# A state-space recurrence in two halves a step, with its outputs half a step late

## Chip, cores and metric

One core of one Trainium2 chip runs the whole program. The metric is device time in microseconds; before the change it was 1826.9 us, the median of three runs (1825.44 to 1828.99).

## What is computed

The layer is a Mamba block followed by a mixture of experts, each with a residual and a layer norm, on 4 sequences of 1024 tokens of width 256, all in float32. Shortened, and with the two norms left as names:

```python
h = rmsnorm(x) @ w_in                          # 256 -> 1024
xs, res = split(h)                             # 512 channels each
res = silu(res)                                # the gate
xs = silu(causal_conv4(xs))
delta, B, C = split(xs @ w_xproj)              # 16, 16 and 16 columns
delta = softplus(delta @ w_dt + b_dt)
# for each channel and each of the 16 states n, along time t:
#   s[t] = exp(delta[t] * A[n]) * s[t-1] + delta[t] * xs[t] * B[n, t]
y = sum over n of s[n] * C[n]
x1 = layernorm(2 * x + ((y + xs * D) * res) @ w_out)
# experts: one shared, and the best 2 of 8 for each token, weighted
out = layernorm(x1 + shared(norm(x1)) + routed(norm(x1)))
```

## The kernel before

The tokens are worked in eight chunks of 512, two to a sequence. Channels lie on partitions: 512 channels are four tiles of 128, so a value for all channels of a chunk is a 128x2048 tile. The loop at the end of the kernel goes over 128 steps, (sequence, chunk, state n). The engines are TensorE (PE), VectorE (DVE), ScalarE (ACT), GpSimd (POOL) and SyncE (SP). A step has four parts, each a small function:

- `over_partitions` (L383): PE copies one row of B or C onto all partitions, in a PSUM tile `pb`.
- `inputs` (L391): ACT copies the B row (`b`, L395); DVE multiplies three of the four channel tiles with it (L397), POOL the fourth (L401). The result is `hs`, of which three buffers exist.
- `scan` (L404): for each channel tile, ACT makes the decay `da` = exp(delta * A) (L409) in one of two PSUM buffers, and DVE runs the scan over time in `hs` (L412). In a sequence's first chunk, ACT then keeps the last column in `state` (L421) for the second.
- `outputs` (L417): DVE multiplies `hs` with the C row in place (L422), and POOL adds the product to `y` (L423).

Around the steps, generators are advanced a piece at a time by `other_work`, which the loop calls twice a step:

- `front` prepares the next chunk: its norm, the projection, the convolution (taps at L302), SiLU of xs (L323), the projections and softplus. Its inner generator `gate` (L280) is started in the chunk's own loop at n = 1; it projects the gate, copies it (L286) and applies SiLU (L288) into `res`, of which there is one buffer.
- `tail` ends a chunk: y times res (L435, on POOL), the output projection (`po`, L446), the layer norm with its square root (`rsqrt`, L194 to L207, twelve small POOL operations after two on DVE), and the router. `by_expert` then sorts the tokens to experts: DVE works out rows and counts in the PSUM tile `pr`; POOL scatters the rows to DRAM by four indirect DMAs for each of a token's two choices (`scatter`, L580 to L592) and makes `there` and `ee` (L609, L611), from which DVE makes a plan of blocks (L615 and after).
- `moe` works off the expert blocks on PE with weights loaded from DRAM by SP: `up` (L748, L755) and `down` (L769, L797), and adds the results to DRAM by POOL's DMAs (L788, L800). Blocks of a chunk are worked during the following chunk's steps; those of the last chunk come after the last step.

The kernel is written in the order of the program; a scheduler then decides each engine's order by what is ready, and pools decide which buffer comes free when. Each engine takes its instructions in order. An ACT function of another table set than the last makes the compiler put a table load ahead of it.

Of the kernel before, what the change touches and what calls it, by code (L numbers as in the profile page):

```python
# [9 lines left out]
AF = mybir.ActivationFunctionType  # L10
# [6 lines left out]
N = 16  # L17
# [5 lines left out]
TC = 512  # L23
NCH = SEQ // TC
TT = TC // P
KD = D // P
KB = DI // P
# [30 lines left out]
def mamba_moe_kernel(  # L58
# [18 lines left out]
    nc = tc.nc  # L77
# [13 lines left out]
    def load_x(b, c):  # L91
        t = two.tile([P, TT, D], F32, tag="x", name=f"x_{b}_{c}", bufs=3)
        nc.sync.dma_start(t, x[b, c * TC : (c + 1) * TC, :].rearrange("(t p) d -> p t d", p=P))
        return t
# [71 lines left out]
    state = const.tile([P, KB, N], F32, tag="state", name="state")  # L166
# [16 lines left out]
    def fill(g):  # L183

        nc.sync.dma_start(sums_of[g][0:P, :], empty[:, 0:D])
        rows = rows_of[g].rearrange("(n p) d -> p n d", p=P)
        for n in range(0, NS // P, 14):
            some = min(14, NS // P - n)
            nc.sync.dma_start(
                rows[:, n : n + some, :], empty.unsqueeze(1).to_broadcast([P, some, W])  # L190
            )
            yield
# [49 lines left out]
    xs_in, gates, scans, channels, routes = {(0, 0): first_x}, {}, {}, {}, {}  # L242
    chunks = [(b, c) for b in range(NSEQ) for c in range(NCH)]
# [4 lines left out]
    def front(b, c):  # L248
# [22 lines left out]
        def projected(m):  # L271
            pi = ps_mix.tile([P, TC], F32, tag="mix", name=f"pi_{s}_{m}")
            for k in range(KD):
                nc.tensor.matmul(  # L274
                    pi, lhsT=w_in_sb[:, k, m * P : (m + 1) * P], rhs=hT[:, k, :],
                    start=(k == 0), stop=(k == KD - 1),
                )
            return pi

        def gate():  # L280

            res = one.tile([P, KB, TC], F32, tag="res", name=f"res_{s}")
            for m in range(KB):
                pi = projected(KB + m)
                yield
                nc.scalar.copy(res[:, m, :], pi)  # L286
                yield
            nc.scalar.activation(res, res, AF.Silu)  # L288
            gates[b, c] = res


        xs = two.tile([P, KB, TC], F32, tag="xs", name=f"xs_{s}")
# [15 lines left out]
        if c > 0:  # L308
            come = one.tile([P, KB, K - 1], F32, tag="come", name=f"come_{s}")
            part = one.tile([P, KB, K - 1], F32, tag="come1", name=f"come1_{s}")  # L310
            for back in range(K - 1, 0, -1):
                to = come if back == K - 1 else part
                nc.gpsimd.tensor_tensor(
                    to[:, :, 0:back], halo[:, :, K - 1 - back :],
                    chan_sb[:, :, CW + K - 1 - back : CW + K - back].to_broadcast([P, KB, back]),
                    ALU.mult,
                )
                if back < K - 1:
                    nc.gpsimd.tensor_tensor(
                        come[:, :, 0:back], come[:, :, 0:back], part[:, :, 0:back], ALU.add  # L320
                    )
            nc.gpsimd.tensor_tensor(xs[:, :, 0 : K - 1], xs[:, :, 0 : K - 1], come, ALU.add)
        nc.scalar.activation(xs, xs, AF.Silu)  # L323


# [53 lines left out]
    def over_partitions(step, row):  # L379

        b, c, n = step
        pb = ps_mix.tile([P, TC], F32, tag="mix", name=f"pb_{b}_{c}_{row}")
        nc.tensor.matmul(  # L383
            pb, lhsT=pick[:, row : row + 1].to_broadcast([P, P]), rhs=scans[b, c][3],
            start=True, stop=True,
        )
        return pb
# [3 lines left out]
    def inputs(step, pb):  # L391
        b, c, n = step
        xs = scans[b, c][0]
        copy = two.tile([P, TC], F32, tag="b", name=f"b_{b}_{c}_{n}")
        nc.scalar.copy(copy, pb)  # L395
        hs = wide.tile([P, KB, TC], F32, tag="s", name=f"hs_{b}_{c}_{n}")
        nc.vector.tensor_tensor(  # L397
            hs[:, 0:on_pool, :], xs[:, 0:on_pool, :],
            pb.unsqueeze(1).to_broadcast([P, on_pool, TC]), ALU.mult,
        )  # L400
        nc.gpsimd.tensor_tensor(hs[:, on_pool, :], xs[:, on_pool, :], copy, ALU.mult)  # L401
        return hs

    def scan(step, hs):  # L404
        b, c, n = step
        delta = scans[b, c][1]
        for k in range(KB):
            da = ps_da.tile([P, TC], F32, tag="da", name=f"da_{b}_{c}_{n}_{k}")
            nc.scalar.activation(  # L409
                da, delta[:, k, :], AF.Exp, scale=chan_sb[:, k, CA + n : CA + n + 1]  # L410
            )
            nc.vector.tensor_tensor_scan(  # L412
                hs[:, k, :], da, hs[:, k, :], 0.0 if c == 0 else state[:, k, n : n + 1],
                ALU.mult, ALU.add,
            )

    def outputs(step, hs, pb):  # L417
        b, c, n = step
        y = scans[b, c][2]
        if c + 1 < NCH:  # L420
            nc.scalar.copy(state[:, :, n : n + 1], hs[:, :, TC - 1 : TC])  # L421
        nc.vector.tensor_tensor(hs, hs, pb.unsqueeze(1).to_broadcast([P, KB, TC]), ALU.mult)  # L422
        nc.gpsimd.tensor_tensor(y, y, hs, ALU.add)  # L423

# [129 lines left out]
    def by_expert(b, c, hn, rank, weights, both, part, flat):  # L554
# [6 lines left out]
        place = part(TT + 1, E)  # L561
# [18 lines left out]
        def scatter(i):  # L580
            nc.gpsimd.tensor_copy(hn[:, :, WEIGHT : WEIGHT + 1], weights[:, i, :].unsqueeze(2))
            for t in range(TT):
                ins = nc.gpsimd.indirect_dma_start(
                    rows_of[g][:, :],
                    bass.IndirectOffsetOnAxis(to[:, i, t : t + 1].bitcast(U32), 0),
                    hn[:, t, :], None,
                ).ins
                for other in scatters:
                    tc.declare_no_dep(ins, other, reason="no two choices share a row")
                for other in taken_from[g]:  # L590
                    tc.declare_no_dep(ins, other, reason="rows behind those of full blocks")
                scatters.append(ins)  # L592

        scatter(0)

        if not at:
            done_of[g] = one.tile([P, E], F32, tag="done", name=f"done_{g}")
# [11 lines left out]
        nc.gpsimd.tensor_tensor(there, there, done, ALU.subtract)  # L609
        ee = one.tile([P, E, E], F32, tag="ee", name=f"ee_{s}")  # L610
        nc.gpsimd.tensor_tensor(ee, before, there.unsqueeze(1).to_broadcast([P, E, E]), ALU.mult)  # L611
        yield
        scatter(1)
        base, ends, first, whose, first_of = part(E), part(E), part(E), part(blocks), part(blocks)
# [5 lines left out]
        of = flat[:, 0 : blocks * E].rearrange("p (a b) -> p a b", a=blocks)  # L620
        step = steps[:, 0:blocks]
# [242 lines left out]
    order = [(b, c, n) for b, c in chunks for n in range(N)]  # L864
    done, beside, work = [], [], moe()
    at_once = 2.0

    def advance(count):
        for _ in range(count):
            if not next(work, False):  # L870
                return False
        return True

    def side():
        for g in list(beside):
            if next(g, "end") == "end":
                beside.remove(g)
        while done:
            beside.append(finish(done.pop(0)))
# [3 lines left out]
    def other_work():  # L883
        nonlocal owed
        side()
        owed += at_once
        while owed >= 1.0:
            owed = owed - 1.0 if advance(1) else 0.0

    for _ in front(0, 0):  # L890
        pass
    xs_in[0, 1] = load_x(0, 1)
    hs = inputs(order[0], over_partitions(order[0], 0))
    for i, step in enumerate(order):
        b, c, n = step
        over_c = over_partitions(step, N + n)
        if i + 1 < len(order) and n + 1 < N:
            over_b = over_partitions(order[i + 1], n + 1)
        scan(step, hs)
        place = chunks.index((b, c))  # L900
        if n == 1:
            beside.append(scans[b, c][4]())
        if n == 2 and place < NGROUP:
            beside.append(fill(place))
        if n == 2 and place + 1 < len(chunks):
            beside.append(front(*chunks[place + 1]))
        other_work()
        if i + 1 < len(order):
            if n + 1 == N:
                over_b = over_partitions(order[i + 1], 0)  # L910
            ahead = inputs(order[i + 1], over_b)
        outputs(step, hs, over_c)
        hs = ahead
        if n == N - 1:
            beside.append(tail(b, c))
            if place + 2 < len(chunks):
                xs_in[chunks[place + 2]] = load_x(*chunks[place + 2])
        other_work()
    working = True
    while working or beside or done:  # L920
        working = next(work, None) is not None
# [56 lines left out]
```

## Time and profile before

| | us |
|---|---|
| median of three runs | 1826.9 |
| profiled execution | 1829.25 |
| its span (first to last instruction) | 1827.6 |
| first scan | 72.5 |
| end of the recurrence, about | 1530 |

The profile is of one execution and gives, per engine, the busy time, groups of instructions by source line, and the waits with the instruction that ended each. The costliest groups, each with its count, busy time and mean of one: L423 (POOL, y) x128, 589.7 us, 4607 ns; L409 (ACT, da) x512, 350.5 us, 696 ns; L412 (DVE, scan) x512, 616.6 us, 1270 ns with a kept state and 1209 ns without; L422 (DVE, C product) x128, 291.9 us, 2280 ns; L397 (DVE, B product) x128, 222.3 us, 1737 ns; L401 (POOL) x128, 176.9 us, 1383 ns. A mean granted PE clock of 0.83 is listed for the core. Idle time counts where it is on the engine that sets the pace of its stretch; elsewhere it costs nothing.

### The profile page before, as it was taken

How to read it: one execution, taken by the hardware profiler on the slowest of the kernel's cores; microseconds unless marked ns; L12 is line 12 of the kernel's file. 1: busy time of each engine (PE TensorE's matmuls, PEld its weight loads, DVE VectorE, ACT ScalarE, POOL GpSimd, SP SyncE). 2: the span in 40 equal slices, each digit the busy share in tenths (PEclk: the TensorE clock that was granted, in tenths of full speed). 3: DMA queues.
4: the chain of work that ended last, by engine and by line, in shares of the span. 5: the costliest groups of instructions: out<-in, count | busy, mean ns of one | idle time of the engine just before them, and what ended most of it. 6: DMA issues, size and time to landing. Idle time of an engine off the chain costs nothing. (4 is left out here: it accounts for less than half of the span.)

```text
span 1827.6 us, 20355 instructions
## 1 busy us (share of the span) xinstructions
PE 1291.5 (71%) x6366; PEld 974.9 (53%) x6366; DVE 1283.7 (70%) x1369; ACT 1118.2 (61%) x2426; POOL 1160.1 (63%) x901
## 2 busy tenths in 40 slices
PE   4354247734788867886887788777887787999970
PEld 1011025512556645674666466655575677899960
DVE  2599898789878877887798778877988795200003
ACT  5555647564758675866686657856785654444433
POOL 1555774688568965896679756976688675412222
PEclk8555567856798978998998889988998898999995
DMA  9990000300055513652175206720653076399985
GB/s 288 321 317 4 0 12 12 124 6 11 15 154 172 156 38 105 204 160 52 51 231 161 78 24 192 216 74 16 199 169 114 27 224 197 103 319 295 316 238 167
DMA packets 199998, 254.19 MB, mean 139 GB/s; under 512 B 21305, under 2 KB 177090, under 8 KB 199890
## 3 DMA queue, kind: packets, MB, share of 16 engines
q1 hardware_dynamic: 173858, 222.54, 37.9%
q0 software_dynamic: 17648, 21.96, 7.0%
q10 hardware_dynamic: 8384, 8.39, 1.3%
q8 instruction: 50, 0.82, 0.2%
q14 instruction: 58, 0.48, 0.1%
HBM read 185.67 MB, written 67.20 MB: 138 GB/s over the span
## 5 line engine op out<-in xcount | busy, mean ns | idle before, releaser
L423 POOL TENSOR_TENSOR y<-y,hs 128x2048 f32<-128x2048 f32 x128 | 589.7, 4607 | 153.1 <-DVE hs L422 150.9
L409 ACT ACTIVATE da<-delta,chan_sb 128x512 f32<-128x512 f32 x512 | 350.5, 696 | 158.6 <-DVE hs L412 154.8
L769 PE MATMUL pd<-w,h 128*128 128x256 f32 x1648 | 403.6, 389 | 24.6 <-ACT rb L797 11.8
L769 PEld LDWEIGHTS pd<-w,h 128*128 128x128 f32 x1648 | 310.4, 195 | 107.6 <-issue 32.4
L412 DVE TENSOR_TENSOR_SCAN hs<-da,state,hs 128x512 f32<-128x512 f32 x256 | 316.4, 1270 | 59.8 <-ACT da L409 58.5
L412 DVE TENSOR_TENSOR_SCAN hs<-da,hs 128x512 f32<-128x512 f32 x256 | 300.2, 1209 | 62.8 <-ACT da L409 62.4
L748 PEld LDWEIGHTS pu<-xT,w 128*128 128x128 f32 x2272 | 287.0, 205 | 65.2 <-ACT xT L734 46.5
L748 PE MATMUL pu<-xT,w 128*128 128x128 f32 x2272 | 292.5, 290 | 38.2 <-ACT xT L734 34.9
L755 ACT ACTIVATE h<-pu,wb 128x128 f32<-128x128 f32 x824 | 236.0, 374 | 105.2 <-PE pu L748 103.0
L422 DVE TENSOR_TENSOR hs<-hs,pb 128x2048 f32<-128x2048 f32 x128 | 291.9, 2280 | 6.7 <-ACT state L421 3.0
L383 PE MATMUL pb<-parts,pick 128*128 128x512 bf16 x256 | 108.8, 440 | 199.4 <-DVE hs L397 78.2
L397 DVE TENSOR_TENSOR hs<-xs,pb 128x1536 f32<-128x1536 f32 x128 | 222.3, 1737 | 31.6 <-POOL xs L374 23.5
L401 POOL TENSOR_TENSOR hs<-xs,b 128x512 f32<-128x512 f32 x128 | 176.9, 1383 | 99.9 <-ACT b L395 99.2
L800 POOL DMA_INDIRECT sums<-rb,xb x71 | 112.9, 1591 | 178.1 <-issue 86.6
L274 PE MATMUL pi<-hT,w_in_sb 128*128 128x512 f32 x256 | 158.4, 754 | 74.1 <-DVE hs L397 25.6
L748 PEld LDWEIGHTS pu<-x1T,w 128*128 128x128 f32 x1024 | 152.6, 230 | 36.3 <-issue 29.8
L748 PE MATMUL pu<-x1T,w 128*128 128x128 f32 x1024 | 156.4, 315 | 1.6 <-ACT h L755 1.3
L213 DVE BATCH_NORM_STATS2 bnst_l<-o 128x6 f32<-128x256 f32 x32 | 11.9, 412 | 192.0 <-DMA o<-sums 192.0
L274 PEld LDWEIGHTS pi<-hT,w_in_sb 128*128 128x128 f32 x256 | 56.1, 234 | 159.4 <-DVE hs L397 44.8
L395 ACT COPY b<-pb 128x512 f32<-128x512 f32 x128 | 74.9, 585 | 79.2 <-PE pb L383 77.9
L383 PEld LDWEIGHTS <-pick 128*128 128x128 bf16 x256 | 26.6, 107 | 154.1 <-issue 110.5
L446 PE MATMUL po<-w_out_sb,y 128*128 128x256 f32 x256 | 74.3, 454 | 44.8 <-POOL y L435 38.2
(160 smaller groups left out, 1434.8 us busy)
## 6 DMA issues: line engine op xcount, KB each, us to landing
w<-in_ew SPq DMA_DIRECT2D x142, 1024.0 KB, 6.0
rows<-empty SPq DMA_DIRECT2D x19, 1806.0 KB, 18.9
w<-in_sw SPq DMA_DIRECT2D x16, 1024.0 KB, 5.7
xb<-rows SPq DMA_DIRECT2D x71, 129.0 KB, 4.7
x<-in_x SPq DMA_DIRECT2D x8, 512.0 KB, 4.5
sums<-summed ACTq DMA_DIRECT2D x8, 512.0 KB, 2.9
sums<-rs POOLq DMA_DIRECT2D x16, 256.0 KB, 4.8
o<-sums SPq DMA_DIRECT2D x4, 1024.0 KB, 8.0
```

What stands on the lines that cost most here:

```text
L274: nc.tensor.matmul(pi, lhsT=w_in_sb[:, k, m * P : (m + 1) * P], rhs=hT[:, k, :], start=(k == 0), stop=(k == KD - 1),)
L383: nc.tensor.matmul(pb, lhsT=pick[:, row : row + 1].to_broadcast([P, P]), rhs=scans[b, c][3], start=True, stop=True,)
L397: nc.vector.tensor_tensor(hs[:, 0:on_pool, :], xs[:, 0:on_pool, :], pb.unsqueeze(1).to_broadcast([P, on_pool, TC]), ALU.mult,)
L401: nc.gpsimd.tensor_tensor(hs[:, on_pool, :], xs[:, on_pool, :], copy, ALU.mult)
L409: nc.scalar.activation(da, delta[:, k, :], AF.Exp, scale=chan_sb[:, k, CA + n : CA + n + 1])
L412: nc.vector.tensor_tensor_scan(hs[:, k, :], da, hs[:, k, :], 0.0 if c == 0 else state[:, k, n : n + 1], ALU.mult, ALU.add,)
L422: nc.vector.tensor_tensor(hs, hs, pb.unsqueeze(1).to_broadcast([P, KB, TC]), ALU.mult)
L423: nc.gpsimd.tensor_tensor(y, y, hs, ALU.add)
L748: nc.tensor.matmul(pu[:, i, :], lhsT=w[:, k, at : at + P], rhs=xT[:, k, :], start=(k == 0), stop=(k == KD - 1),)
L755: nc.scalar.activation(t[:, i, :], pu[:, i, :], AF.Relu, bias=wb[:, m : m + 1])
L769: nc.tensor.matmul(pd, lhsT=hidden[h][:, i, :], rhs=w[:, m, :], start=(m == 0), stop=(m == HB - 1 and e is None),)
L800: nc.gpsimd.indirect_dma_start(sums_of[g][:, :], bass.IndirectOffsetOnAxis(xb[:, TOKEN : TOKEN + 1].bitcast(U32), 0), rb, None, compute_op ...
```

## The change

A step's scans are split in two: channel tiles 0 and 1, then 2 and 3. Between the halves stand the outputs of the step before, and the first call of other work; the C row is asked for after that call. After the second half the state is kept, the next step's inputs are made, and the second call of other work follows. A chunk's tail and the load of a later x move from the end of the chunk's last step into the first step of the next chunk.

SiLU of the gate leaves `gate` (except for the last chunk) and is written in the following chunk's `front`, directly ahead of SiLU of xs. In `by_expert`, the first `scatter` is written after `there` and `ee`.

```diff
         def gate():
...
-            nc.scalar.activation(res, res, AF.Silu)
             gates[b, c] = res
+            if (b, c) == chunks[-1]:
+                nc.scalar.activation(res, res, AF.Silu)
...
+        place = chunks.index((b, c))
+        if place:
+            gate_before = gates[chunks[place - 1]]
+            nc.scalar.activation(gate_before, gate_before, AF.Silu)
         nc.scalar.activation(xs, xs, AF.Silu)
...
-    def scan(step, hs):
+    def scan(step, hs, of):
...
-        for k in range(KB):
+        for k in of:
...
+    def keep(step, hs):
+        b, c, n = step
+        if c + 1 < NCH:
+            nc.scalar.copy(state[:, :, n : n + 1], hs[:, :, TC - 1 : TC])
+
     def outputs(step, hs, pb):
...
-        if c + 1 < NCH:
-            nc.scalar.copy(state[:, :, n : n + 1], hs[:, :, TC - 1 : TC])
...
-        scatter(0)
...
         nc.gpsimd.tensor_tensor(ee, before, there.unsqueeze(1).to_broadcast([P, E, E]), ALU.mult)
+        scatter(0)
         yield
         scatter(1)
...
+    first, second = range(KB // 2), range(KB // 2, KB)
+    hs, late = inputs(order[0], over_partitions(order[0], 0)), None
     for i, step in enumerate(order):
         b, c, n = step
-        over_c = over_partitions(step, N + n)
-        if i + 1 < len(order) and n + 1 < N:
+        place = chunks.index((b, c))
+        more = i + 1 < len(order)
+        if more and n + 1 < N:
             over_b = over_partitions(order[i + 1], n + 1)
-        scan(step, hs)
-        place = chunks.index((b, c))
+        scan(step, hs, first)
+        if late is not None:
+            outputs(*late)
+            if n == 0:
+                beside.append(tail(*chunks[place - 1]))
+                if place + 1 < len(chunks):
+                    xs_in[chunks[place + 1]] = load_x(*chunks[place + 1])
...
         other_work()
-        if i + 1 < len(order):
-            if n + 1 == N:
-                over_b = over_partitions(order[i + 1], 0)
-            ahead = inputs(order[i + 1], over_b)
-        outputs(step, hs, over_c)
-        hs = ahead
-        if n == N - 1:
-            beside.append(tail(b, c))
-            if place + 2 < len(chunks):
-                xs_in[chunks[place + 2]] = load_x(*chunks[place + 2])
+        over_c = over_partitions(step, N + n)
+        if more and n + 1 == N:
+            over_b = over_partitions(order[i + 1], 0)
+        scan(step, hs, second)
+        keep(step, hs)
+        late = (step, hs, over_c)
+        if more:
+            hs = inputs(order[i + 1], over_b)
         other_work()
+    outputs(*late)
+    beside.append(tail(*chunks[-1]))
```

More of the change, by code (lines that the diff above doesn't have):

```diff
@@ L892, in mamba_moe_kernel @@
     xs_in[0, 1] = load_x(0, 1)
-    hs = inputs(order[0], over_partitions(order[0], 0))
+    first, second = range(KB // 2), range(KB // 2, KB)
+    hs, late = inputs(order[0], over_partitions(order[0], 0)), None
     for i, step in enumerate(order):
         b, c, n = step
-        over_c = over_partitions(step, N + n)
-        if i + 1 < len(order) and n + 1 < N:
+        place = chunks.index((b, c))
+        more = i + 1 < len(order)
+        if more and n + 1 < N:
             over_b = over_partitions(order[i + 1], n + 1)
-        scan(step, hs)
-        place = chunks.index((b, c))
+        scan(step, hs, first)
[5 more added lines that the diff above has]
+                    xs_in[chunks[place + 1]] = load_x(*chunks[place + 1])
         if n == 1:
```

## The prediction

> **What bounds the kernel now.** I read the page's busy shares first, then the busy time by stretch, to see where one engine sets the pace.
>
> ```profile
> span 1827.6 us, 20355 instructions
> ...
> PE 1291.5 (71%) x6366; PEld 974.9 (53%) x6366; DVE 1283.7 (70%) x1369; ACT 1118.2 (61%) x2426; POOL 1160.1 (63%) x901
> ```
>
> No engine looks full over the whole span, but the stretches differ (columns: stretch, its length, then busy PE, PEld, DVE, ACT, POOL, with the PE clock, DMA share and GB/s last):
>
> ```profile
> 72.50:1530.00 1457.50, 1033.62 (x4804) 752.21 (x4803) 1237.47 (x1220) 960.83 (x1991) 1062.29 (x725) 0.82 0.38 112
> 1530.00:1827.00 297.00, 232.16 (x1518) 213.38 (x1518) 29.04 (x119) 116.95 (x360) 73.57 (x121) 0.89 0.76 234
> ```
>
> In the recurrence (72.5 to 1530 us) DVE works 1237.5 of 1457.5 us. One of the 128 steps is four scans, a B product and a C product: 4 x 1.24 + 1.74 + 2.28 = 8.98 us of DVE, 1149 us in all; the rest is the next chunk's convolution and the routing. The last 297 us belong to the expert blocks, PE and weight DMAs, and the change adds or removes nothing there. So the time is DVE's work plus 220 us of DVE idle. Next come DVE's waits in that stretch (total us, times, longest):
>
> ```profile
> DVE hs L412 <- ACT da L409: 120.8, 59, 4.8
> DVE pr L615 <- POOL ee L611: 41.2, 7, 6.1
> DVE half_l L198 <- POOL var L463: 9.5, 6, 2.0
> DVE hs L397 <- POOL xs L374: 8.7, 2, 4.4
> ```
>
> Two waits are three quarters of the idle time: scans waiting for their exponents, and one small reduction per chunk waiting for POOL. Why it waits is in POOL's timeline (start, duration):
>
> ```profile
> 695.74 4.54 POOL L423 TENSOR_TENSOR y<-y,hs 128x2048 f32<-128x2048 f32 x1
> 700.44 1.06 POOL L583 DMA_INDIRECT rows<-hn,to  x1 [0.16 <-DVE hs L412]
> 701.80 0.99 POOL L583 DMA_INDIRECT rows<-hn,to  x1 [0.30 <-issue]
> 703.10 0.97 POOL L583 DMA_INDIRECT rows<-hn,to  x1 [0.30 <-issue]
> 704.37 0.97 POOL L583 DMA_INDIRECT rows<-hn,to  x1 [0.30 <-issue]
> 705.36 0.22 POOL L609 TENSOR_TENSOR there<-there,done 128x8 f32<-128x8 f32 x1
> 705.66 0.32 POOL L611 TENSOR_TENSOR ee<-before,there 128x64 f32<-128x64 f32 x1
> ```
>
> `ee` stands behind an addition to y and four scatters. DVE, in order, sits 5.65 us at L615 with scans queued behind it. ACT's own waits name a third party:
>
> ```profile
> ACT da L409 <- DVE hs L412: 154.8, 202, 4.4
> ACT hn L236 <- POOL shift_n L234: 32.2, 7, 5.6
> ACT hn L263 <- POOL root_r L206: 15.0, 6, 5.4
> ```
>
> The first is the two-buffer exchange of exponents; the others are POOL's chain of tiny square-root instructions, and every exponent queued behind such a wait is late. One 5.5 us wait (833.5 to 839.1) leads directly to a 4.77 us DVE stall at 843.2.
>
> **What the Trainium skill says.** "Perfetto Trace Analysis", Optimization Strategy: find the gaps on the most contended engine within its regime and who ends them; it adds that a repeating gap can mean too few buffers. The trace agrees: the gaps repeat by chunk, and `da` has two buffers. "GPSIMD Engine Reference", 3.1, gives 4497 ns on POOL and 2293 ns on DVE for a 2048-wide f32 addition; the rows here have 4607 and, for the product, 2280 ns. "ScalarE: Activation LUTs", What ACT_TABLE_LOAD costs, puts 1283 ns of load and 1380 ns of drain on a switch; the trace shows the 1283 ns, but the next activation starts 1.29 us after the load (908.72 to 910.01), so I price a switch at 1.28.
>
> **The change, part by part.** Where code leaves the order to the scheduler I read the instruction order of both built programs.
>
> *Scatter behind ee.* In six of seven chunks `there` and `ee` now stand behind one and two scatters, and POOL's addition ahead of them is an older one, 6 to 9 us of DVE work earlier. From the scatter's indices to `ee`: 2 x 1.3 + 0.25 + 0.3 + 0.35 = 3.5 us. DVE has meanwhile a 0.41 reduction, two taps of 0.74 and a C product of 2.28: 4.2 us, so the wait goes. In the seventh (chunk 7's loop) only 1.74 us stands between and the wait stays. 6 x 5.85 = **-35 us**. Scatters landing late cost nothing: the block rows they feed come after four shared units on PE, over 30 us.
>
> *Halves.* Exponents 0, 1 and 2, 3 are now queued with other ACT work between the pairs, and DVE has a wide product beside it. I tallied the queues: for each exponent, the ACT work queued since the previous one (table load 1.28, 2048-wide 1.91, 512-wide 0.58 to 0.70, 256-wide 0.50, 128-wide 0.30), plus its own 0.69, against two scans less 0.69 (1.8 us) and whatever else DVE has between. The excess is a stall. Before, it sums to 101 us where the trace has 120.8; after, to 67, scaled by 1.2 to 80: **-41 us**. Example: in odd chunks the SiLU of xs stands in a 6.6 us block ahead of the third exponent of step 9 (2.0 allowed: 5.3 over); after, that block falls where a wide product covers most of it. The C-row product on PE moves with it and is wanted half a step later: 9 us of cover for a 0.44 us matmul.
>
> *What the new order makes late.* The tally knows no waits on POOL. Walking steps 2 to 5 through the queues with the rows' durations: at step 3 the third exponent stands behind L263, which needs POOL's first chain. That chain is now split by a scatter (1.6 + 0.3) and a slice of hs (1.3) and starts after the late addition (4.6); L263 is released about 6.8 us after the root's start, ACT then needs 4 us, DVE has 4.2 us of work: a stall of 6.7 us, of which the tally holds 3.8. Then `half_l` comes 2.7 us after the C product, and the addition that follows that product holds POOL for 4.6 and `var` 0.9: 2.8 us of wait against 1.6 now. About 4.5 us a chunk in six chunks: **+28 us**. Bounds: 0 if POOL is ahead of my walk, +60 if each of the two waits grows to the longest seen (5.5).
>
> *SiLU adjacent.* In the built order the two SiLUs stand apart in all seven chunks, since the gate's is ready earlier and gets hoisted. ACT's table loads go from 72 to 70: 2.6 us of ACT time, which is not on the path: 0. Had it worked, 14 loads or 18 us of ACT, inside waits: 0 to -15.
>
> *The rest.* Same instruction counts on DVE; state copies move ahead of the next inputs, ACT 0.2 us each behind a scan that the next exponents await anyway: 0 (up to +6, 64 x 0.1). x's load is issued half a step later on SP; it lands in 4.5 us and is read 1.5 steps (15 us) later: 0. The gate's buffer is freed by the y-times-res product half a step later; walked, ACT reaches its first copy as POOL ends it: 0, up to +1 a chunk. The last chunk's tail follows one more call of expert work, which PE has to do in any case: 0, up to +5.
>
> Sum: -35 - 41 + 28 = **-48 us**. The profiled execution took 1829.25 us (span 1827.6 and 1.65 around it), 2.35 above the median of three, 1826.9. 1829.25 - 48 - 2.35 = 1779.
>
> **Rivals.** *All of it arrives* (0.2): POOL's chain stays ahead, so -76 or somewhat more: 1750. For it: POOL idles 27% of the recurrence. Against: at steps 2 to 4 POOL is what ACT already waits for (32.2 us). *Only the routing wait goes* (0.15): half of the tally's gain is eaten by waits that it doesn't know, -35 - 20 + 28 = -27: 1800. For it: DVE is already 85% busy there and PE reaches 83%. *Slower* (0.11): ACT's in-order wait for POOL's square-root results, now ahead of the second pair of exponents. Each step between 2 and 5 that catches such a wait costs 6.7 us of DVE; the change is a loss once new stalls pass 76 / 7 = 11 us a chunk, thus from two full waits a chunk beyond today's: 2 x 6.7 x 7 = 94, net +18: 1845. Against it: one of the two is already walked at only 2.9 beyond the tally. *It does not do what it says*: the scheduler hoists C products and SiLUs, so DVE's order in many steps is as before; if the exponent stalls then stay too, that is the second rival.
>
> **How the numbers follow.** My own case has 0.5, no change 0.04. Faster: 0.5 + 0.2 + 0.15 = 0.85; slower 0.11. About 0.2% (3.7 us) is what a measurement of this kernel can tell from no change. The range runs from the full gain with a little more (-85: 1742) to the smallest gain with its unknowns (-12: 1815); it leaves out the slower case, no change and a small part below. Likeliest: 1779.
>
> **What would show it.** Right: L615's successor waits under 8 us in the recurrence; the scans' wait on `da` falls to about 80 us; DVE busy unchanged at 1237, its idle time near 170; new: a wait of 5 us or more of L263 on POOL at step 3, and `half_l` on `var` near 20 us in all. Wrong: the wait on `da` stays at 120 or grows, with POOL's roots as ACT's releaser; or ACT's table loads fall by 14.

## The result, and the profile after

The changed kernel takes **1833.9 us** (median of 20 runs, 1825.5 to 1844.3) where the kernel before took 1826.7 beside it (20 runs, 1823.5 to 1833.3). The ratio is 1.0038, 95% interval 1.0022 to 1.0054: **slower**, by some 7 us, where 48 less were forecast. The profiled execution after took 1841.0 us, 7 above its median; the spans of the two executions shown differ by 11.7.

The page after, its span and its busy times:

```profile
span 1839.3 us, 20307 instructions
...
PE 1313.3 (71%) x6365; PEld 983.6 (53%) x6366; DVE 1290.8 (70%) x1369; ACT 1110.6 (60%) x2424; POOL 1160.5 (63%) x901
```

The same work on every engine, in a little more time. The recurrence and the end, by stretch (stretch, length, busy PE, PEld, DVE, ACT, POOL, then PE clock, DMA share, GB/s):

```profile
72.00:1535.00 1463.00, 1052.14 (x4786) 758.04 (x4786) 1242.36 (x1219) 951.84 (x1987) 1060.39 (x724) 0.81 0.37 110
1535.00:1840.00 305.00, 235.80 (x1536) 216.22 (x1535) 30.36 (x120) 117.73 (x362) 74.84 (x122) 0.89 0.76 232
```

From the first scan to the last, the recurrence took 1462.7 us, 8.3 more than before; the rest of the 11.7 lies behind it. DVE is idle for 216 us of the recurrence, as before (215): the idle time did not shrink, it moved. DVE's waits in that stretch (us in total, times, longest) follow. An edit shifts line numbers, so the exponents `da` are L409 before, L416 here and L411 or L414 in the experiments:

```profile
DVE hs L419 <- ACT da L416: 111.9, 51, 7.6
DVE hs L404 <- ACT b L402: 23.7, 16, 5.2
DVE half_l L198 <- POOL var L473: 13.9, 6, 2.8
DVE hs L404 <- POOL y L433: 12.2, 9, 2.4
DVE xs L304 <- ACT xs L298: 10.2, 5, 3.4
DVE hs L432 <- ACT state L427: 10.2, 5, 4.5
DVE hs L432 <- PE pb L390: 9.8, 6, 2.3
DVE pr L625 <- POOL ee L620: 4.7, 1, 4.7
```

The wait for `ee` went from 41.2 to 4.7, the scans' wait for exponents from 120.8 only to 111.9. All other waits together went from 53 to 99: the next B product waits for the copy `b` and for POOL to free its buffer, the C product for the `state` copy and for `pb`. PE's clock was a little lower here (0.81 for 0.82), which explains little: DVE's waits for PE grew only from 12.8 to 14.1 us in all, and ACT's wait for the matmul that copies a B row fell from 77.9 to 32.8. ACT's own waits name what stands in its queue:

```profile
ACT da L416 <- DVE hs L419: 151.2, 167, 6.4
ACT res L287 <- POOL y L445: 39.9, 7, 6.8
ACT hn L236 <- POOL shift_n L234: 37.4, 7, 7.1
...
ACT hn L263 <- POOL root_r L206: 30.0, 6, 6.9
```

The second line is new: before, the copies into `res` waited for PE and never for POOL:

```profile
ACT res L286 <- PE pi L274: 36.7, 12, 6.5
```

L263 is ACT's scaling of the next chunk's x for its norm: the first instruction that needs the square root which POOL's chain of small operations makes. Its line has doubled (15.0 before). Both can be followed in the timeline of one chunk, steps 1 to 3 (start, duration, and in brackets how long its engine was idle ahead of it and for what):

```profile
795.61 4.51 POOL L445 TENSOR_TENSOR y<-y,res 128x2048 f32<-128x2048 f32 x1
...
800.15 0.58 ACT L287 COPY res<-pi 128x512 f32<-128x512 f32 x1 [4.98 <-POOL y L445]
...
802.49 2.34 DVE L419 TENSOR_TENSOR_SCAN hs<-da,hs 128x512 f32<-128x512 f32 x2 [2.92 <-ACT da L416]
...
818.90 0.51 ACT L263 ACTIVATE hn<-x,root_r 128x256 f32<-128x256 f32 x1 [6.57 <-POOL root_r L206]
...
822.73 1.22 DVE L419 TENSOR_TENSOR_SCAN hs<-da,hs 128x512 f32<-128x512 f32 x1 [6.23 <-ACT da L416]
...
831.59 0.17 DVE L198 TENSOR_SCALAR half_l<-var 128x8 int32<-128x8 int32 x1 [2.75 <-POOL var L473]
```

Read it in pairs. POOL multiplies y by res until 800.1; ACT's copy of the next gate into the one `res` buffer waits 4.98 us for that; the exponent queued behind the copy is late and DVE loses 2.92. Then L263 waits 6.57 us for POOL's roots and DVE loses 6.23. At 831.6 `half_l`, the first instruction of the tail's square root on DVE, loses 2.75.

Adding up the idle times in brackets of DVE's timeline between the first scans of the steps named, over all chunks, gives the table that the rest of this text uses (us; the first two rows are this comparison, the others are experiments below). Each row is one execution; that of the changed kernel took 7 us more than its median and that of the halves alone 5 less, so small differences between rows mean nothing:

| | steps 0-3 | 4-7 | 8-11 | 12-15 | all |
|---|---|---|---|---|---|
| before | 26.4 | 68.0 | 68.1 | 52.7 | 215.2 |
| after | 70.1 | 49.5 | 44.9 | 51.4 | 216.0 |
| halves alone | 70.8 | 55.9 | 49.1 | 58.0 | 233.8 |
| halves, front earlier | 24.0 | 54.7 | 57.9 | 49.2 | 185.8 |
| before, front earlier | 37.2 | 105.6 | 32.0 | 53.8 | 228.6 |

After step 3 the change saves 43 us of idle time. In steps 0 to 3 it loses 44.

### The profile page after: what moved, and what is told of

It is laid out like the page before. It is cut to its first block, busy times and chain, and to the rows that moved or that the text cites. A ratio compares the mean times of both kernels' runs of the same rounds, so it can differ in the third digit from the quotient of the medians.

```text
span 1839.3 us, 20307 instructions
## 1 busy us (share of the span) xinstructions
PE 1313.3 (71%) x6365; PEld 983.6 (53%) x6366; DVE 1290.8 (70%) x1369; ACT 1110.6 (60%) x2424; POOL 1160.5 (63%) x901
## 5 line engine op out<-in xcount | busy, mean ns | idle before, releaser
L416 ACT ACTIVATE da<-delta,chan_sb 128x512 f32<-128x512 f32 x512 | 348.0, 694 | 152.7 <-DVE hs L419 151.2
L779 PE MATMUL pd<-w,h 128*128 128x256 f32 x1648 | 398.5, 389 | 24.1 <-ACT rs L793 9.7
L758 PE MATMUL pu<-xT,w 128*128 128x128 f32 x2272 | 300.0, 292 | 17.1 <-ACT xT L744 12.8
L390 PE MATMUL pb<-parts,pick 128*128 128x512 bf16 x255 | 113.6, 451 | 194.9 <-DVE hs L404 111.8
L408 POOL TENSOR_TENSOR hs<-xs,b 128x512 f32<-128x512 f32 x128 | 180.8, 1417 | 84.7 <-ACT b L402 83.3
L274 PE MATMUL pi<-hT,w_in_sb 128*128 128x512 f32 x256 | 177.6, 830 | 69.2 <-DVE hs L432 43.7
L758 PEld LDWEIGHTS pu<-x1T,w 128*128 128x128 f32 x1024 | 142.7, 217 | 36.2 <-issue 29.1
L758 PE MATMUL pu<-x1T,w 128*128 128x128 f32 x1024 | 147.0, 303 | 3.2 <-ACT h L765 3.2
L274 PEld LDWEIGHTS pi<-hT,w_in_sb 128*128 128x128 f32 x256 | 60.6, 257 | 165.4 <-DVE hs L432 62.8
L456 PE MATMUL po<-w_out_sb,y 128*128 128x256 f32 x256 | 77.3, 468 | 32.8 <-ACT res L287 27.8
L456 PEld LDWEIGHTS po<-w_out_sb,y 128*128 128x128 f32 x256 | 60.9, 242 | 63.8 <-ACT res L287 30.4
```

What stands on the lines that cost most here:

```text
L274: nc.tensor.matmul(pi, lhsT=w_in_sb[:, k, m * P : (m + 1) * P], rhs=hT[:, k, :], start=(k == 0), stop=(k == KD - 1),)
L390: nc.tensor.matmul(pb, lhsT=pick[:, row : row + 1].to_broadcast([P, P]), rhs=scans[b, c][3], start=True, stop=True,)
L416: nc.scalar.activation(da, delta[:, k, :], AF.Exp, scale=chan_sb[:, k, CA + n : CA + n + 1])
L456: nc.tensor.matmul(po[:, i, :], lhsT=y[:, k, t * P : (t + 1) * P], rhs=w_out_sb[:, k, :], start=(k == 0), stop=(k == KB - 1),)
L758: nc.tensor.matmul(pu[:, i, :], lhsT=w[:, k, at : at + P], rhs=xT[:, k, :], start=(k == 0), stop=(k == KD - 1),)
L779: nc.tensor.matmul(pd, lhsT=hidden[h][:, i, :], rhs=w[:, m, :], start=(m == 0), stop=(m == HB - 1 and e is None),)
```

## Experiments

The theories: **A**, the halves lose through POOL: its late additions delay the root chain and the freeing of `res`, and ACT waits for these ahead of the second pair of exponents. **B**, the halves lose because other ACT work stands between the pairs, whatever it waits for. All times are medians of 4 to 22 runs, the ratio is to the kernel before on the same chip (1827.0 to 1827.7).

| kernel | us | ratio (95% interval) |
|---|---|---|
| moved scatter alone | 1815.0 | 0.9936 (0.9918 to 0.9955) |
| moved SiLU alone | 1810.4 | 0.9904 (0.9884 to 0.9924) |
| scatter and SiLU | 1797.0 | 0.9834 (0.9810 to 0.9859) |
| halves alone | 1857.8 | 1.0164 (1.0142 to 1.0186) |
| halves and scatter | 1850.2 | 1.0116 (1.0095 to 1.0138) |
| halves, one Newton step | 1797.7 | 0.9849 (0.9823 to 0.9876) |
| before, one Newton step | 1780.5 | 0.9734 (0.9713 to 0.9756) |
| halves, work after the pairs | 1841.9 | 1.0079 (1.0055 to 1.0103) |
| halves, outputs as before | 1852.5 | 1.0142 (1.0119 to 1.0166) |
| halves, var on DVE | 1857.7 | 1.0165 (1.0143 to 1.0187) |
| halves, gate later | 1836.3 | 1.0048 (1.0031 to 1.0066) |
| before, gate later | 1860.5 | 1.0178 (1.0164 to 1.0193) |
| after, gate later | 1826.9 | 0.9995 (0.9988 to 1.0003) |
| halves, front earlier | 1808.2 | 0.9892 (0.9871 to 0.9914) |
| before, front earlier | 1853.9 | 1.0144 (1.0128 to 1.0161) |
| after, front earlier | 1815.8 | 0.9929 (0.9915 to 0.9944) |
| halves, front earlier, one Newton step | 1765.9 | 0.9666 (0.9653 to 0.9679) |
| scatter, SiLU, two Newton steps | 1755.5 | 0.9606 (0.9593 to 0.9620) |

### The three edits apart

Each of the change's three parts on the kernel before, and halves with the scatter.

*Scatter alone:*

```diff
-        scatter(0)
...
         nc.gpsimd.tensor_tensor(ee, before, there.unsqueeze(1).to_broadcast([P, E, E]), ALU.mult)
+        scatter(0)
         yield
```

> The kernel before with one edit: the first four scatters are written after there and ee. In POOL's built order one scatter instead of four now stands ahead of ee, so ee comes about 3.9 us earlier in each of the seven chunks inside the recurrence; everything else keeps its order. Theory A (stalls of VectorE add up, a removed one stays removed): VectorE's wait on ee falls from 41 to about 15 us and the time falls by 20 to 27 us, to about 1803. Theory B (the removed stall is given back at the next wait, since the exponents or POOL are late there in any case): the wait on ee falls likewise, but the time falls by less than 8 us.

Measured: 12.6 us less. POOL's timeline in one chunk shows why it is not 36:

```profile
880.87 4.54 POOL L423 TENSOR_TENSOR y<-y,hs 128x2048 f32<-128x2048 f32 x1
885.35 0.22 POOL L607 TENSOR_TENSOR there<-there,done 128x8 f32<-128x8 f32 x1
885.72 1.04 POOL L583 DMA_INDIRECT rows<-hn,to  x1
886.78 0.34 POOL L609 TENSOR_TENSOR ee<-before,there 128x64 f32<-128x64 f32 x1
```

One scatter is still ahead of `ee` and so is the addition to y, so DVE waits 28.6 us in all for `ee`, from 41.2. That is 12.6 less, and so is the time: here the removed wait stayed removed, as theory A of the expectation has it, but it was half of what that counted on. Only with the halves, whose addition is an older one, does it fall to 4.7.

*SiLU alone:* the gate's SiLU leaves `gate` and is written ahead of that of xs, as in the change.

> The kernel before with one edit: SiLU of the gate is written in the next chunk's front, ahead of SiLU of xs. Table loads go from 72 to 70 in the built order. Both theories: within 4 us of before. A loss of more than 6 us would put the blame for the whole result on this edit.

Measured: 17 us less. ACT's table loads are 70 for 72, as in the changed kernel, and the two SiLUs stand apart here too. What counts is where the gate's SiLU stands. Before, in one chunk's step 5:

```profile
851.83 1.28 ACT L288 ACT_TABLE_LOAD   x1
853.12 1.91 ACT L288 ACTIVATE res<-res 128x2048 f32<-128x2048 f32 x1
855.05 1.28 ACT L409 ACT_TABLE_LOAD   x1
...
857.14 1.22 DVE L412 TENSOR_TENSOR_SCAN hs<-da,hs 128x512 f32<-128x512 f32 x1 [3.63 <-ACT da L409]
```

and with the SiLU moved, in the same chunk:

```profile
841.77 1.28 ACT L327 ACT_TABLE_LOAD   x1
842.52 2.33 DVE L417 TENSOR_TENSOR_SCAN hs<-da,hs 128x512 f32<-128x512 f32 x2
843.07 1.91 ACT L327 ACTIVATE res<-res 128x2048 f32<-128x2048 f32 x1
...
845.10 2.29 DVE L427 TENSOR_TENSOR hs<-hs,pb 128x2048 f32<-128x2048 f32 x1 [0.25 <-ACT state L426]
```

The block of 4.47 us stood between the second and third exponent of a step and cost DVE 3.63; now it stands behind the step's last exponent, beside two scans and a C product, and costs 0.25. The scans' wait for exponents fell from 120.8 to 106.5 us. The load is 1.28 us, as the Trainium skill has it ("ScalarE: Activation LUTs", What ACT_TABLE_LOAD costs); of the 1.38 us of drain that it adds nothing shows: SiLU starts 1.29 and 1.30 us after the load did.

*Halves alone*, and *halves with the scatter*: the changed kernel with the other edits undone.

> The changed kernel without the moved scatter and without the moved SiLU: only the two halves and the late outputs. Theory A: this part by itself loses 20 to 35 us, through the stall at step 3 (exponents behind L263's wait for POOL's root, 6 us), the wait of half_l (2.8 us) and the gate's copy behind the y-times-res product (3 us), and the moved scatter hides that loss in the whole change. Theory B: it is within 10 us of before, like the whole change.

> The changed kernel without the moved SiLU. Theory A and B: within 4 us of the whole change (1834), as the SiLU is hoisted in either case. If it is below before by more than 5 us, the moved SiLU is what turned a gain into a loss.

Measured: the halves alone cost 30 us; the scatter takes 8 of them back, the SiLU 16 more (to 1833.9). DVE's waits with the halves alone:

```profile
DVE hs L414 <- ACT da L411: 124.5, 51, 6.2
DVE xs L303 <- ACT xs L297: 15.6, 9, 4.8
DVE pr L621 <- issue: 14.8, 5, 4.6
```

The exponents' wait, which the halves were to cut by 41 us, is 124.5: it did not fall at all. The fall to 111.9 in the changed kernel came with the moved SiLU (with the halves and the scatter it is 134.5). In chunks 3 to 6, where DVE idles 13.8 us in steps 0 to 3, four stalls make up 13.4 of it: B product on POOL 1.6, scan behind the copy into res 2.9, scan behind L263 6.2, `half_l` 2.7.

*Scatter and SiLU without the halves:*

> The kernel before with the moved scatter and the moved SiLU of the gate, and no halves. If the two gains add up (12.6 and 17.2 us alone), 1827.6 - 30 = 1798, and the whole change at 1834 is then these two less about 36 us for the halves. If both pay from the same wait (each delays or frees the same stretch of steps 5 to 9), 1808 to 1812.

Measured: 1797.0; the two gains add up (12.6 and 17.2 make 29.8; measured 30.0). This beats both kernels with the same arithmetic.

### Is it POOL's root chain?

One Newton step in place of three, in every square root, on the halves and on the kernel before (8 of a root's 12 small POOL operations left out):

```diff
-        for _ in range(3):
+        for _ in range(1):
             nc.gpsimd.tensor_tensor(t, y, y, ALU.mult)
```

> The halves alone, with one Newton step in each square root instead of three (8 of the 12 small POOL operations left out, so the roots are coarser). Theory A, the halves lose because POOL's root chain now starts behind the late addition to y and ACT's queue waits for it ahead of the second pair of exponents: the idle time of DVE in steps 0 to 3 falls from 13.8 us a chunk by about 5, and the time from 1857.8 to 1820 to 1830. Theory B, the halves lose because two pairs of exponents with other ACT work between leave the scans less lead, whatever POOL does: 1850 or more, da's wait still about 120 us.

> The kernel before, with one Newton step in each square root instead of three. With the halves this took 60 us: 16 of them after the recurrence (the last layer norm's roots), 36 in it. Theory A, the halves lose because they put POOL's root chain in ACT's way: here the recurrence gains 5 to 15 and the end 16, so 1796 to 1806, and with the short chain the halves cost nothing or little (1797.65). If the chain is a cost of both kernels alike, the recurrence gains 36 here too: about 1775, and the halves still lose 23 to 25.

Measured: -60 us with the halves, and -47 on the kernel before. In the executions profiled the recurrence, from the first scan to the last, became 34 us shorter with the halves (1479.7 to 1445.2 us) and 30 without (1454.5 to 1424.2); the stretch behind it became 16 and 15 shorter, of which the last layer norm's four roots are 9. So the chain is dear in both kernels, and its length explains 13 of the 30 us that the halves lose. Theory A in this form falls: it gave the kernel before 5 to 15 us in the recurrence. A shorter chain takes the exponents' wait to about 89 us in both. But steps 0 to 3, where the gain was expected, lose 64.3 us with the halves still, from 70.8. The scan behind L263 no longer waits there; the next B product does instead:

```profile
826.67 1.75 DVE L399 TENSOR_TENSOR hs<-xs,pb 128x1536 f32<-128x1536 f32 x1 [3.71 <-ACT b L397]
```

Of a stall of 6.2 us, 3.7 came back within the same step, and the gain lies mostly in steps 4 to 7 (55.9 to 38.2). Theory B's 1850 or more falls too: the same work between the pairs, waited for a shorter time, costs far less.

Two more ways to part A from B. *Work after*: the first call of other work goes behind the second pair of scans, outputs still late. *Outputs before*: the pairs are kept with other work between them, but a step's outputs stand at its end, as before.

```diff
+        over_c = over_partitions(step, N + n)
+        if more and n + 1 == N:
+            over_b = over_partitions(order[i + 1], 0)
+        scan(step, hs, second)
+        keep(step, hs)
         if n == 1:
             beside.append(scans[b, c][4]())
...
         other_work()
-        over_c = over_partitions(step, N + n)
...
-        scan(step, hs, second)
-        keep(step, hs)
```

> Halves, with the first call of other work behind the second pair of scans and ahead of the next inputs, where the kernel before has it; the outputs stay half a step late between the pairs. Theory A: the root's users no longer stand ahead of the second pair, so the 6.2 us stall at step 3 goes, while POOL's late addition still delays half_l by some 2.7 us a chunk: about 1830. Theory B (it is the other work between the pairs, of whatever kind, that makes scans wait): also 1830 or less, with da's wait spread back to where the kernel before has it. A third theory, that it is the late outputs alone: stays near 1858.

> Halves of the scans with the first call of other work between them, but the outputs at the end of the step as in the kernel before, the next inputs ahead of them. Theory A: POOL's addition is out of the way of the root chain as before, so L263's wait on POOL falls from some 6 us to 3 or less a time, and half_l's below 2: about 1835. Theory B: other work still stands between the pairs and DVE has no wide product there to cover it: 1858 or more.

Measured: -16 and -5: neither is one theory's number. With the work after the pairs the exponents' wait falls to 77 us, but C products then wait 32 us for the state copy and the taps 28. Step 3 loses 45 us over all chunks, more than the 39 of the halves alone (11.5 before): its scans still wait some 4.5 us in four chunks, and B products wait 15.7 us for `b`. Neither the late outputs nor the work between the pairs is the loss by itself.

*var on DVE*, with the three small operations ahead of `half_l` moved off POOL:

```diff
-        nc.gpsimd.tensor_scalar(var[:, 0, :], mv[:, :, 1], 1.0, 1e-5, ALU.mult, ALU.add)
+        nc.vector.tensor_scalar(var[:, 0, :], mv[:, :, 1], 1.0, 1e-5, ALU.mult, ALU.add)
```

> Halves, with the three small operations that make var on DVE instead of POOL, so half_l no longer stands behind POOL's late addition to y. DVE has 3 x 0.17 us more a chunk and loses a wait of 2.7 us in five chunks, and the tail's root starts earlier: -10 to -15, about 1845. If the wait only passes on to the next instruction: 1855 or more.

Measured: no gain. The wait of `half_l` for POOL is gone and DVE's idle time fell by 15 us (233.8 to 219.0), but DVE's busy time in the recurrence grew by 18: the small operations themselves now last until POOL's addition is over (start, duration):

```profile
455.36 4.51 POOL L428 TENSOR_TENSOR y<-y,hs 128x2048 f32<-128x2048 f32 x1
456.49 3.41 DVE L468 TENSOR_TENSOR var<-var,mv 128x4 f32<-128x4 f32 x1
```

455.36 + 4.51 = 459.87, and 456.49 + 3.41 = 459.90. The wait was not taken away; it moved inside an instruction, where no view calls it a wait (see the last section).

### When gate and front start

*Gate later*: the gate starts at n = 2, on the halves and on both kernels.

```diff
-        if n == 1:
+        if n == 2:
             beside.append(scans[b, c][4]())
```

> Halves, with the gate started one step later (n = 2 for n = 1), so that its first copy into res no longer meets y times res of the chunk before. If that copy's wait on POOL (39.8 us of ACT in seven chunks) is what stalls DVE by 2.9 us in step 1 or 2 of each chunk: about -17, 1840. If ACT would wait for da's buffers in that time anyway: 1855 or more.

> The kernel before with the gate started at n = 2 for n = 1, as it gave the halves 21 us. If that was the collision of res with the late product of the chunk before, which is the halves' own: no gain here, 1820 to 1835, since no copy into res waits for POOL in the kernel before. If it is only that gate work lies better one step later: -15 to -20, about 1808.

> The whole change, with the gate started a step later. If res meets y times res here as in the halves (39.9 us of ACT's waits): 1834 - 21 = 1813. If the moved SiLU of the gate, which holds res longer, has made this wait harmless: 1834.

Measured: -21 with the halves, **+33** on the kernel before, -7 on the whole change, between the two forecasts. With the halves and with the whole change the copies into `res` no longer wait for POOL at all. DVE's first wait with the halves is

```profile
DVE hs L414 <- ACT da L411: 73.4, 50, 5.9
```

from 124.5: below the 80 that was forecast. The stall of a scan behind the copy (2.9) is gone and that behind L263 is 3.0 instead of 6.2, at the price of new waits in steps 4 to 7 (67.8 us for 55.9). This is the plainest answer to the prediction: the exponents' wait is 47 us below that of the kernel before, more than the 41 that were forecast, and DVE is idle for 214.6 us, where the kernel before has 215.2. On the kernel before the same edit runs into other work:

```profile
DVE hs L422 <- PE pb L383: 28.7, 5, 6.3
DVE hs L397 <- ACT b L395: 14.6, 11, 3.3
DVE hs L422 <- ACT res L288: 13.2, 2, 6.6
```

The gate's SiLU now holds a C product up, and the row copies stand behind the gate's matmuls. So n = 1 fits the old order of steps, and is a step too early for the new one.

*Front earlier*: the next chunk's front starts in the second call of step 1 instead of the first of step 2.

```diff
-        if n == 2 and place + 1 < len(chunks):
-            beside.append(front(*chunks[place + 1]))
...
+        if n == 1 and place + 1 < len(chunks):
+            beside.append(front(*chunks[place + 1]))
         other_work()
```

> Halves, with the next chunk's front started half a step earlier, in the second call of step 1. In the built order this brings the root chain and its user L263 ahead by most of a chunk, to steps 9 to 11 of the chunk before, away from L287 and the tail's root. Theory A: step 3 loses its 6.2 us stall, 1857.8 - 30 = about 1828, if the chain's new place has no scans behind it. Theory B (ACT's work between the pairs, whatever it waits for): the work only moves, 1850 or more.

> The kernel before with the front started half a step earlier, as it gave the halves 50 us. In its built order the root chain stays behind the addition of step 1, since the tail's tile in the rowset pool still comes first there, while in the halves it moves ahead of it. If the halves' loss is the place of the front against the late outputs and the late tail: within 10 us of 1827. If an earlier front is good for both: 1800 or less.

> The whole change, with the front half a step earlier. If the 50 us of the halves alone add up with the other two edits: 1834 - 50 = 1784, near the 1779 that was predicted for the change. If the moved SiLU and scatter had hidden part of the same stalls: 1795 to 1810.

Measured: **-50** with the halves, **+26** on the kernel before, -18 on the whole change. With the halves, the root chain and L263 now come in the chunk before, from the fourth chunk on in its step 10:

```profile
719.08 0.91 ACT L263 ACTIVATE hn<-x,root_r 128x256 f32<-128x256 f32 x2 [5.47 <-POOL root_r L206]
```

Step 3 of the next chunk begins at 811. ACT still waits 5.5 us for the roots, but at this place DVE loses at most 0.6 us in the step. Steps 0 to 3 fall from 70.8 to 24.0 us of idle time, and the exponents' wait falls in all to half of what it was in the kernel before:

```profile
DVE hs L414 <- ACT da L411: 60.0, 39, 5.7
DVE pr L621 <- POOL ee L617: 37.2, 6, 6.3
```

On the kernel before, the chain stays where it was, and the front's other work collides in steps 4 to 7 (105.6 us of idle time for 68.0). Why the chain can come so early in one order and not in the other was not settled; the reason that the expectation gave, the order in the rowset pool, was not tested by itself. The place of the side work against the steps is thus worth more than the edit under study, and it has the opposite sign for the two orders. The three edits do not add up, either: with the scatter and the SiLU as well, the earlier front brings 18 and not 50 (1815.8, where the halves with it alone are at 1808.2). There the wait for `ee` is 26.0 us, not the 4.7 of the changed kernel, and the exponents' 80.7.

That leaves the two theories so: A named the right places, since moving the work away from them pays most, but the 30 us do not divide into shares of a cause. Shorter roots take 13 of them, a later gate 21 and an earlier front 50, each for itself. B does not hold: with the same work between the pairs, started half a step earlier, the halves are 19 us faster than the kernel before.

### What is left of the halves, and the best version

*Halves, front earlier, one Newton step*, to be held against the kernel before with one Newton step; and *scatter, SiLU, two Newton steps*, without halves.

> Halves with the front half a step earlier and one Newton step in each root instead of three (8 of 12 small POOL operations left out). If the halves have a gain of their own (the prediction's 41 us), it shows against the kernel before with the same short roots, 1780.5: about 1755 to 1765, as 1808 less 45 to 50. If the earlier front had already taken out what short roots take out: 1780 to 1790, and the halves are worth nothing.

> The kernel before with the moved scatter and SiLU and two Newton steps for three (4 of 12 small POOL operations left out of each root; two steps from this start still give some 5e-6 of relative error). One step for three took 46.6 us from the kernel before, so half of it: 1797 - 23 = about 1774. If POOL's chain was hidden behind the moved scatter: 1790 to 1797.

Measured: 1765.9 against 1780.5 for the kernel before with the same roots. Out of the two collisions' way the halves gain about 15 us here and 19 with full roots (1808.2 against 1827), not 41. And 1755.5 for the last, 41 less than with three Newton steps where 23 were expected, the best of all. In its trace DVE idles 155 us in the recurrence, for 192 with three steps; but the trace of the latter is of its slowest execution (1808.2 us, 11 above the median), so that part of the 37 is noise.

## Why the prediction was wrong

Of the signs that were named ahead, the wait for `ee` (4.7 us) and L263's long wait at step 3 came. The exponents' wait near 80 and DVE's idle time near 170 did not: they were 111.9 and 216.

**The scatter behind ee (-35): the wait right, the gain not.** The wait fell by 36.5 us, in the chunks named, and stayed in the last (4.7). But it fell so far only with the halves, whose addition ahead of it is an older one: with these alone it is 20.1 us already. By itself the move brought 13 us, and next to the halves 8. Beside the halves, the waits of that reduction fell by 15 us (20.1 to 4.7) and the exponents' wait grew by 10 (124.5 to 134.5): in these two executions, 1.3 us apart, what DVE no longer lost there it lost again, most of it at scans (idle 233.8 and 233.5).

**Halves (-41): the step that failed.** The tally counted what stands ahead of each exponent and took a shorter wait for exponents as shorter time. First, ACT's queue also carries `b`, the state copy, xs for the taps and, through POOL, the buffers that DVE's wide products need. Work moved away from exponents was moved ahead of these. DVE's waits other than those for `da` and `ee` grew by 46 us in the changed kernel and by 36 with the halves alone, where the forecast had about 7 for `half_l`. Second, the exponents' wait fell by 9 where 41 was forecast, and that came with the moved SiLU, which stood in the order that was tallied; with the halves alone it rose by 4. Where it did fall as forecast (73.4, gate later), DVE's idle time stayed that of the kernel before. Third, the tally held DVE's busy time fixed, and with the halves alone 7 us of the 25 by which the recurrence is longer are busy time (last section). The halves measured by themselves are +30; with the side work started to fit them they are -19 against the kernel before. So a gain exists, at half its price, and only with another start of the side work.

**What the new order makes late (+28): right in the places, short in the sum.** The two stalls that were walked came as walked: 6.7 us forecast behind L263 at step 3 and 6.23 measured, though in four chunks and not six, 2.8 for `half_l` and 2.75 measured. (The term's own parts, 2.9 and 1.2 beyond what was counted already, make 25 us in six chunks, not 28.) The term walked steps 2 to 5 only, and left out two stalls of steps 1 and 2: the copy into res and the B product that waits for POOL. Steps 0 to 3 lost 44 us more than before.

**The gate's buffer ("0, up to +1 a chunk"): 3 us a chunk.** The walk had ACT reach its first copy as POOL ends y times res; ACT came 5 us sooner. The gate started a step later gives the halves 21 us back. The Trainium skill ("Perfetto Trace Analysis", Optimization Strategy) says that a gap repeating on the engine that should be full can mean too few buffers. This gap fits: `res` has one buffer, and the copy waits for POOL seven times, once for each chunk that has one before it. That a second buffer would close it was not tried; a later first copy did.

**SiLU adjacent (0): -17.** The forecast that the two stand apart and the loads go from 72 to 70 held; the price did not. It looked at ACT's busy time, which is not on the path, and not at the exponents queued behind the SiLU, for which the scans wait.

**The rivals.** The slower one named ACT's in-order waits for POOL ahead of the second pair, which is what steps 1 to 3 show, and put its threshold at 11 us of new stalls a chunk. New stalls measured about 9 us a chunk in steps 0 to 3 of chunks 3 to 6, below that threshold; it was a loss all the same, since the threshold was set against gains of 76 us and the later steps saved 43. So its side and place were right, its sum was not. Its mechanism is not the whole loss: short roots help the kernel before almost as much. The two faster rivals counted on the tally's gain, or on half of it, and fail with it.

## What to carry to other kernels

- Where one engine's idle time is a chain of in-order hand-overs, a stall that is removed is not a gain until it is known what that engine does next. Walk the queue to the end of the period, with every kind of instruction that the supplying engine feeds, not only the one whose wait is the largest.
- Side work that is issued at fixed places among the steps is tuned to the order of the steps. When the steps are shifted by half, shift its starts too and measure both orders with both starts: here the same one-line moves were worth -21 and -50 us in one order and +33 and +26 in the other.
- Measure the parts of a change apart. Two of three were worth 30 us together and hid that the third cost as much.
- Count an engine's busy time again after a change of order, even with the same instructions: part of a wait can sit inside an instruction.

## What the runs showed of the hardware

A small operation on DVE can last until an addition on POOL ends. `half_r`, the first instruction of the front's square root on DVE, has four elements a partition. One tile's view (minimum, median, maximum, in ns), of the kernel before and of the halves alone:

```profile
L198 DVE TENSOR_SCALAR half_r<-ms x8: 150/177/1075, 7.0 to 1202.0; 128x4 int32<-128x4 int32 x8
L198 DVE TENSOR_SCALAR half_r<-ms x8: 157/1095/3954, 6.9 to 1211.4; 128x4 int32<-128x4 int32 x8
```

In the changed kernel it starts while POOL adds to y:

```profile
807.16 4.95 POOL L433 TENSOR_TENSOR y<-y,hs 128x2048 f32<-128x2048 f32 x1
...
810.93 1.23 DVE L198 TENSOR_SCALAR half_r<-ms 128x4 int32<-128x4 int32 x1 [0.21 <-ACT ms L258]
```

Both end at 812.1. In all six chunks in whose steps it stands, in the changed kernel and in the halves alone, `half_r` ends 0.02 to 0.05 us after such an addition, and with var on DVE so does one of the var operations in chunks 2 to 6. The Trainium skill ("SBUF — State Buffer", Who interferes with whom) says why: an operation of this kind on DVE can need the pair of ports that it shares with POOL, and whoever comes second is blocked until the first ends. The ends agree with that; no run here took the port away to prove it. The profile counts the time as busy: `half_r` went from 2.6 to 10.1 us in the recurrence of the changed kernel and of the halves alone, which is all of the 7 us by which DVE's busy time grew there. The forecast that it would not change missed it. Other orders pay it too: with the outputs as before, `half_r` and the instruction after it hold DVE 18 us longer than in the kernel before, and in the kernel before with the gate later `half_r` alone 10. Scans and wide products, with a PSUM operand each, keep their 1.2, 1.7 and 2.3 us beside the same additions.
